# Half tiles for the last rows of an expert in a two-layer transformer kernel

## The chip, the core and the metric

The kernel runs on one core of a Trainium2 chip, as one launch. The metric is the device time of one execution in microseconds (us); the median of three executions stands for a kernel. One further execution was taken with the hardware profiler, and every row of a profile below is from that one.

TensorE is written PE (PEld is its loading of weights, which overlaps its matmuls), VectorE DVE, ScalarE ACT, GpSimd POOL, and SP is the engine that only issues DMAs. All data are float32, and a float32 matmul shows in the profile as two passes.

## The reference

Two sequences of 2048 tokens with 256 features go through two layers. What matters here is the mixture of experts in layer 0, which sees the normalised tokens `xn`:

```python
scores = softmax(x @ gate_w + gate_b)                 # 8 experts
weights, indices = top_k(scores, 2)                   # two experts for each token
p1 = x @ rw1[e] + rb1[e]                              # 256 -> 512, for each chosen expert e
p2 = x @ rw2[e] + rb2[e]
routed_e = (silu(p1) * p2) @ rw3[e] + rb3[e]          # 512 -> 256
out = shared(x) + sum(weights * routed_e over the two chosen)
```

Around it stand a causal attention of layer 0, two shared experts of the same form, and in layer 1 another causal attention and a block that works on 255 chosen tokens of each sequence. There are 4096 tokens, so 8192 pairs of a token and an expert; how many fall to one expert depends on the data.

## The kernel before

**Layer 0's attention, with side work.** `attention` goes over 32 blocks of 128 query rows. Scores are made by L251 and scaled by DVE in L262, the exponential is ACT's L270, POOL splits each row into two 16-bit planes (L301), SP transposes them by DMA (L303, tile `across`), DVE and ACT join them again (L281, L282), and L316 multiplies by the values. Beside it runs side work, a generator: each `yield` in it is one step, and `beside()` takes steps at a set rate per piece of attention. `behind` ties POOL's DMAs of the side work to DVE's last main instruction, so that they don't come in a burst. The DMAs that clear buffers in DRAM (`clear`, issued by ACT at L420 to L442, biases packed last) are taken one or two per block of rows.

**Planning (`route_experts`, side work).** DVE finds the two best experts of each token. Two matmuls (L537, L538) count the rows of each expert. From the counts (`many`, `last`, L549 to L557) each expert gets `ceil(rows / 256)` tiles of `TT = 256` rows, one behind the other in a DRAM buffer `sorted_x`, and each pair gets its place there (`place`, L565). `tile_expert` (L574) holds the expert of each tile, and `filled` (L575) the number of tiles. Then 64 indirect DMAs of POOL (L580) scatter the tokens' rows to their places.

**Expert tiles (`fetch` and `run`).** At most `NT = 39` tiles can be needed. `LIKELY = 36` of them are run always, the other 3 in one block under `tc.If(used > LIKELY)` (L773). For each tile `fetch` has SP load the tile's expert number into a register (L622), transpose the tile's rows from DRAM (L626, `xs`), and load the expert's weights (L631, three `rw` tiles of 512 KB) and biases (L635, `be`), whatever expert the tile before had. These tiles have two buffers each, and `chained` keeps SP's DMAs of all tiles in one order. `run` then has POOL put the two 16-bit halves together (L730, `xT`), multiplies into `ps_sc` and `ps_tr` (L737: two groups `h`, in each two matmuls per 128 hidden features and projection), applies Silu on ACT (L745), multiplies on DVE (L746, `hid`), multiplies by the third weight (L752: two blocks of 128 rows, four matmuls each), adds the bias (L757, `y`) and stores to `sorted_y` (L758). From the twelfth tile on ACT loads one later weight behind each tile (L767), and behind one of the last tiles four small products for layer 1 are made (L706).

**After the tiles** come the shared experts (L1370, L1389) with the gathering of the routed rows from `sorted_y` by indirect DMA (L1359), then layer 1.

## Time and profile before

| | us |
|---|---|
| three executions | 1529.97, 1533.32, 1532.8 |
| their median | 1532.8 |
| profiled execution, its own time | 1530.43 |
| its span on the core | 1528.7 |
| PE busy | 1474.6 |
| first matmul of the expert tiles to the first of the shared experts | 378.5 |

The span is the stretch from the first to the last recorded instruction; the rest of an execution's time lies around it. The mean granted clock of PE is 0.996 of full. In groups of instructions a matmul's length covers its way through the array, and the next one starts before it ends; what counts for PE is the distance from start to start. A row of DMAs gives the size of one and the median time from issue to landing:

```profile
rw<-in_rw SPq DMA_DIRECT2D x108, 512.0 KB, 4.3
be<-biases SPq DMA_DIRECT2D x36, 132.0 KB, 4.2
xs<-sorted_x SPq DMA_TRANSPOSE x36, 3.4
```

### The profile page before, as it was taken

What the parts mean: (1) busy time and instruction counts of PE and PEld (TensorE: products, weight loads), DVE (VectorE), ACT (ScalarE), POOL (GpSimd) and SP (SyncE); (2) the same over time, 40 slices, a digit from 0 to 9 for tenths busy, and PEclk for the clock granted to TensorE, in tenths of its full rate; (3) what the DMA queues carried; (4) which work ended last, traced back from release to release, by engine and by line L of the source; (5) the groups of instructions that cost most, each with busy time, mean ns of one, the idle gap of its engine ahead of it and who ended that gap; (6) DMA issues with size and microseconds to landing.
All of it is one profiled execution on the core that took longest, in us unless ns stands there. A gap on an engine that the chain in (4) does not pass through costs nothing.

```text
span 1528.7 us, 17889 instructions
## 1 busy us (share of the span) xinstructions
PE 1474.6 (96%) x5828; PEld 1047.4 (69%) x5828; DVE 698.3 (46%) x2055; ACT 442.1 (29%) x831; POOL 409.4 (27%) x596
## 2 busy tenths in 40 slices
PE   7999999999999999999999999999999998999998
PEld 4566666568888888888556566566675765676665
DVE  6446333342222222222334446767546458666344
ACT  2443343341111111111121211115623532354233
POOL 3555776431111111110112220132012122421132
PEclk9999999999999999999999999999999999999999
DMA  4944765656888879874110110130005435621144
GB/s 150 268 107 116 174 137 134 158 119 175 212 218 231 238 234 270 237 202 122 30 40 28 42 42 21 37 135 28 1 14 111 109 67 114 151 52 23 35 114 103
DMA packets 290558, 183.49 MB, mean 120 GB/s; under 512 B 192960, under 2 KB 265408, under 8 KB 290464
## 3 DMA queue, kind: packets, MB, share of 16 engines
q1 hardware_dynamic: 255168, 134.95, 35.7%
q10 hardware_dynamic: 27664, 26.53, 5.5%
q0 software_dynamic: 7632, 20.86, 4.4%
q8 instruction: 47, 0.77, 0.2%
q14 instruction: 47, 0.39, 0.1%
HBM read 93.14 MB, written 45.14 MB: 90 GB/s over the span
## 4 chain that ended last, share of the span: by engine, by line
PE 28%; issue 9%; DVE 7%; POOL 3%; DMA 3%; ACT 2%; SPq 0%; POOLq 0%; ACTq 0%; DVEq 0%
PE ps_tr L1370 6%; PE ps_sc L1370 6%; PE ps_pv L1389 5%; POOL planes L301 3%; DMA across<-planes 2%; PE ps_mm L1241 2%; PE ps_mm L1203 1%; DVE x L1400 1%; PE ps_sc L251 1%; PE ps_mm L833 1%; PE ps_mm L1224 1%; PE ps_pv L316 1%; PE ps_tr L251 1%; PE ps_mm L1307 1%; DVE row L262 1%
## 5 line engine op out<-in xcount | busy, mean ns | idle before, releaser
L301 POOL COPY planes<-row 128x512 uint16<-128x512 uint16 (+3 forms) x320 | 166.6, 565 | 304.9 <-ACT row L270 279.1
L282 ACT COPY pT<-across 128x512 uint16<-128x512 uint16 (+3 forms) x160 | 105.9, 676 | 214.7 <-DMA across<-planes 204.5
L251 PE MATMUL ps_sc<-xnT,qT 128*128 128x512 f32 (+3 forms) x384 | 161.6, 542 | 0.1
L746 DVE SCALAR_TENSOR_TENSOR hid<-ps_tr,be,act 128x256 f32<-128x256 f32 x144 | 63.1, 480 | 197.9 <-PE ps_tr L737 188.9
L745 ACT ACTIVATE act<-ps_sc,be 128x256 f32<-128x256 f32 x144 | 60.5, 471 | 302.0 <-PE ps_sc L737 302.0
L1359 POOL DMA_INDIRECT ya<-sorted_y,place x64 | 62.3, 974 | 308.1 <-DVE x L1400 224.7
L737 PE MATMUL ps_sc<-xT,rw 128*128 128x256 f32 x576 | 136.2, 379 | 1.6 <-POOL xT L730 1.6
L737 PE MATMUL ps_tr<-xT,rw 128*128 128x256 f32 x576 | 136.1, 379 | 0.0
L316 PE MATMUL ps_pv<-v,pT 128*128 128x256 f32 x544 | 129.6, 384 | 5.9 <-ACT pT L282 4.5
L730 POOL COPY xT<-xs 128x512 uint16<-128x512 uint16 x72 | 51.3, 758 | 309.7 <-DMA xs<-sorted_x 269.9
L752 PE MATMUL ps_pv<-rw,hid 128*128 128x256 f32 x576 | 132.0, 382 | 0.0
L316 PE MATMUL ps_pv<-vg,pT 128*128 128x256 f32 x544 | 124.9, 380 | 5.0 <-ACT pT L282 4.9
L1370 PE MATMUL ps_tr<-xnT,sw 128*128 128x512 f32 x256 | 122.0, 593 | 0.0
L1370 PE MATMUL ps_sc<-xnT,sw 128*128 128x512 f32 x256 | 121.9, 594 | 0.1
L316 PEld LDWEIGHTS ps_pv<-vg,pT 128*128 128x128 f32 x544 | 101.5, 189 | 28.9 <-ACT pT L282 9.5
L316 PEld LDWEIGHTS ps_pv<-v,pT 128*128 128x128 f32 x544 | 101.7, 191 | 28.3 <-ACT pT L282 8.4
L737 PEld LDWEIGHTS ps_sc<-xT,rw 128*128 128x128 f32 x576 | 109.4, 190 | 16.8 <-POOL xT L730 2.0
L737 PEld LDWEIGHTS ps_tr<-xT,rw 128*128 128x128 f32 x576 | 109.4, 190 | 14.9
L752 PEld LDWEIGHTS ps_pv<-rw,hid 128*128 128x128 f32 x576 | 104.9, 189 | 21.2 <-DVE hid L746 6.6
L1389 PE MATMUL ps_pv<-sw,hid 128*128 128x256 f32 x512 | 117.7, 380 | 0.0
L1389 PEld LDWEIGHTS ps_pv<-sw,hid 128*128 128x128 f32 x512 | 96.5, 190 | 19.1 <-issue 6.2
L251 PEld LDWEIGHTS ps_sc<-xnT,qT 128*128 128x128 f32 x384 | 70.4, 191 | 53.6 <-issue 43.3
(319 smaller groups left out, 1936.1 us busy)
## 6 DMA issues: line engine op xcount, KB each, us to landing
rw<-in_rw SPq DMA_DIRECT2D x108, 512.0 KB, 4.3
sorted_x<-zero ACTq DMA_DIRECT2D x13, 768.0 KB, 6.5
sorted_y<-y SPq DMA_DIRECT2D x36, 256.0 KB, 4.3
be<-biases SPq DMA_DIRECT2D x36, 132.0 KB, 4.2
table<-xn SPq DMA_DIRECT2D x8, 514.0 KB, 3.4
x<-in_x SPq DMA_DIRECT2D x8, 512.0 KB, 6.7
gains<-zero ACTq DMA_DIRECT2D x8, 512.0 KB, 3.4
gain<-gains SPq DMA_DIRECT2D x16, 256.0 KB, 2.7
```

The source lines that it names most:

```text
L251: product = nc.tensor.matmul(ps[:, :w], lhsT=qT[:, dc, (i % 4) * P : (i % 4 + 1) * P], rhs=xnT[g0 + k][:, dc, :w], start=(dc == 0), stop=( ...
L282: nc.scalar.copy(words[:, :, 0], flat[:, w : 2 * w]),
L301: nc.gpsimd.tensor_copy(planes[:, h * w : (h + 1) * w], halves[:, :, 1 - h])
L316: product = nc.tensor.matmul(pv[:, :D], lhsT=turned[k][:, j : j + P], rhs=values[g0 + k][:, j // P, :D], start=(c + j == 0), stop=(c + j = ...
L730: nc.gpsimd.tensor_copy(words[:, :, :, 1 - k], xs[:, 2 * k : 2 * k + 2, :])
L737: nc.tensor.matmul(ps[:, k * TT : (k + 1) * TT], lhsT=we_in[:, dc, (h + k) * P : (h + k + 1) * P], rhs=xT[:, dc, :], start=(dc == 0), stop ...
L745: activated = nc.scalar.activation(act, p1[:, at], AF.Silu, bias=b1[:, hc])
L746: nc.vector.scalar_tensor_tensor(hid[:, h + k, :], p2[:, at], b2[:, hc], act, op0=ALU.add, op1=ALU.mult)
L752: product = nc.tensor.matmul(po[:, r, :], lhsT=hid[:, hc, r * P : (r + 1) * P], rhs=w3[:, hc, :], start=(hc == 0), stop=(hc == 3),)
L1359: nc.gpsimd.indirect_dma_start(out=ya, out_offset=None, in_=sorted_y, in_offset=bass.IndirectOffsetOnAxis(ap=place[rank][:, t : t + 1], ax ...
L1370: product = nc.tensor.matmul(ps, lhsT=ww[:, dc, hc * P : (hc + 1) * P], rhs=xnT[g][:, dc, :], start=(dc == 0), stop=(dc == 1),)
L1389: product = nc.tensor.matmul(po[:, :D], lhsT=hid[:, hc, j * P : (j + 1) * P], rhs=w["sw3", n][:, hc, :], start=(hc == 0), stop=(hc == 3),)
```

## The change

An expert's rows are cut into whole tiles of 256; a remainder of more than 128 rows gets a whole tile, and one of 1 to 128 rows gets a half tile of `HT = 128`. Whole tiles come first in `sorted_x`, half tiles behind all of them from row `NT * TT`. At most 35 whole and 8 half tiles can be needed; the buffers keep their 9984 rows. 32 whole and 4 half tiles are run always, the half ones behind the 5th, 13th, 21st and 29th whole one. The 3 other whole and 4 other half tiles stand in one conditional block, which runs all seven if there are more than 32 whole or more than 4 half tiles. A half tile runs the same instructions on 128 columns, with one block of rows in place of two at the third weight; its weights and biases are loaded in full. Planning gets the instructions that find the half tiles and move their rows' places, and one more `yield`; clearing `sorted_y` takes two DMAs where it took one.

```diff
-NT = (2 * B * S + E * (TT - 1)) // TT
-LIKELY = 2 * B * S // TT + E // 2
+HT = TT // 2
+NT, NH = (2 * B * S + E * (HT - 1)) // TT, E
+LIKELY, LIKELY_H = 2 * B * S // TT, E // 2
+PLACES = NT * TT + NH * HT
...
-            for r in range(LIKELY * TT, NT * TT, step):
+            for r, end in ((LIKELY * TT, NT * TT), (NT * TT + LIKELY_H * HT, PLACES)):
...
-            nc.vector.tensor_sub(many, at[:, 1:], at[:, :E])
-            nc.vector.tensor_scalar(
-                many, many, 1.0 / TT, (TT - 1.0) / TT - 0.5 + 0.5 / TT, op0=ALU.mult, op1=ALU.add
-            )
+            nc.vector.tensor_sub(count, at[:, 1:], at[:, :E])
+            nc.vector.tensor_scalar(many, count, 1.0 / TT, -0.5 / TT, op0=ALU.mult, op1=ALU.add)
...
+            nc.vector.scalar_tensor_tensor(half, many, -float(TT), count, op0=ALU.mult, op1=ALU.add)
+            nc.vector.tensor_scalar(half, half, 0.0, None, op0=ALU.is_gt)
             nc.vector.tensor_tensor_scan(last, many, many, 0.0, ALU.add, ALU.max)
+            nc.vector.tensor_tensor_scan(half_last, half, half, 0.0, ALU.add, ALU.max)
+            nc.vector.tensor_sub(jump, half_last, half)
+            nc.vector.tensor_scalar(jump, jump, float(HT), float(NT * TT), op0=ALU.mult, op1=ALU.add)
+            nc.vector.scalar_tensor_tensor(jump, last, -float(TT), jump, op0=ALU.mult, op1=ALU.add)
...
+            nc.vector.tensor_scalar(count, last, float(TT), None, op0=ALU.mult)
...
+            yield
+            nc.vector.tensor_tensor(total, summed, each_expert(count), ALU.is_ge)
+            nc.vector.tensor_tensor(total, total, each_expert(jump), ALU.mult)
+            nc.vector.tensor_tensor(summed, summed, total, ALU.add)
...
-            nc.vector.tensor_copy(filled, last[:, E - 1 :])
+            nc.vector.tensor_scalar(one[:, 0:1], last[:, E - 1 :], -float(LIKELY), 0.0, op0=ALU.add, op1=ALU.max)
+            nc.vector.tensor_scalar(one[:, 1:2], half_last[:, E - 1 :], -float(LIKELY_H), None, op0=ALU.add)
+            nc.vector.tensor_tensor(filled, one[:, 0:1], one[:, 1:2], ALU.max)
...
+        def place_of(t):
+            return (t * TT, TT) if t < NT else (NT * TT + (t - NT) * HT, HT)
...
-            part = slice(t * TT, (t + 1) * TT)
+            first, n = place_of(t)
...
-                                ps[:, k * TT : (k + 1) * TT],
+                                ps[:, k * n : (k + 1) * n],
...
-            for r in range(2):
+            r_n = n // P
+            for r in range(r_n):
...
-        for t in range(LIKELY):
+        every_so = LIKELY // LIKELY_H
+        planned = []
+        for t in range(LIKELY):
+            planned.append(t)
+            if t % every_so == every_so // 2:
+                planned.append(NT + t // every_so)
+        for at, t in enumerate(planned):
             product, activated = run(t)
...
-        with tc.If(used > LIKELY):
-            for t in range(LIKELY, NT):
+        with tc.If(used > 0):
+            for t in [*range(LIKELY, NT), *range(NT + LIKELY_H, NT + NH)]:
                 run(t)
```

More of the change, by code (lines that the diff above doesn't have):

```diff
@@ L54, in transformer_kernel @@
     dram = ctx.enter_context(tc.tile_pool(name="scratch", bufs=2, space=bass.MemoryType.DRAM))
-    sorted_x = dram.tile([NT * TT, 2 * D], U16, tag="sorted_x", name="sorted_x", bufs=1)
-    sorted_y = dram.tile([NT * TT, D], F32, tag="sorted_y", name="sorted_y", bufs=1)
+    sorted_x = dram.tile([PLACES, 2 * D], U16, tag="sorted_x", name="sorted_x", bufs=1)
+    sorted_y = dram.tile([PLACES, D], F32, tag="sorted_y", name="sorted_y", bufs=1)
     gains = [dram.tile([S + 1, D], F32, tag=f"gains{b}", name=f"gains{b}", bufs=1) for b in range(B)]
@@ L353, in transformer_kernel @@
     gate = [keep_pool.tile([P, NB * 4], F32, tag=f"gate{k}", name=f"gate{k}") for k in range(2)]
-    tile_expert = keep_pool.tile([P, NT], I32, tag="tile_expert", name="tile_expert")
+    tile_expert = keep_pool.tile([P, NT + NH], I32, tag="tile_expert", name="tile_expert")
     filled = keep_pool.tile([P, 1], I32, tag="filled", name="filled")
@@ L418, in clear @@
             step = 3 * TT
-            for r in range(0, NT * TT, step):
+            for r in range(0, PLACES, step):
                 yield nc.scalar.dma_start(
@@ L423, in clear @@
                 )
-            for r in range(LIKELY * TT, NT * TT, step):
+            for r, end in ((LIKELY * TT, NT * TT), (NT * TT + LIKELY_H * HT, PLACES)):
                 yield nc.scalar.dma_start(
-                    sorted_y[r : r + step, :].rearrange("(p r) d -> p r d", p=P),
-                    zero.bitcast(F32).unsqueeze(1).to_broadcast([P, step // P, D]),
+                    sorted_y[r:end, :].rearrange("(p r) d -> p r d", p=P),
+                    zero.bitcast(F32).unsqueeze(1).to_broadcast([P, (end - r) // P, D]),
                 )
@@ L546, in route_experts @@
             nc.vector.tensor_copy(at[:, 1:], summed[:, :, n - 1])
-            many, last = (plan.tile([P, E], F32, tag=t, name=t) for t in ("many", "last"))
-            nc.vector.tensor_sub(many, at[:, 1:], at[:, :E])
-            nc.vector.tensor_scalar(
-                many, many, 1.0 / TT, (TT - 1.0) / TT - 0.5 + 0.5 / TT, op0=ALU.mult, op1=ALU.add
-            )
+            count, many, last, half, half_last, jump = (
+                plan.tile([P, E], F32, tag=t, name=t) for t in ("count", "many", "last", "half", "half_last", "jump")
+            )
@@ L558, in route_experts, with each_expert @@
             nc.vector.tensor_sub(sflat, sflat, tflat)
             nc.vector.tensor_tensor(sflat, sflat, ps[:, : E * n], ALU.add)
-            nc.vector.tensor_tensor(summed, summed, many.unsqueeze(2).to_broadcast([P, E, n]), ALU.add)
+            def each_expert(t):
+                return t.unsqueeze(2).to_broadcast([P, E, n])
+            nc.vector.tensor_tensor(summed, summed, each_expert(many), ALU.add)
+            yield
+            nc.vector.tensor_tensor(total, summed, each_expert(count), ALU.is_ge)
@@ L565, in route_experts @@
                 nc.vector.tensor_copy(place[rank], one)
-            tiles = plan.tile([P, NT, E], F32, tag="tiles", name="tiles")
-            nc.gpsimd.iota(
-                tiles, pattern=[[1, NT], [0, E]], base=0, channel_multiplier=0, allow_small_or_imprecise_dtypes=True
-            )
-            nc.vector.tensor_tensor(tiles, tiles, last.unsqueeze(1).to_broadcast([P, NT, E]), ALU.is_ge)
-            whose = plan.tile([P, NT], F32, tag="whose", name="whose")
+            tiles = plan.tile([P, NT + NH, E], F32, tag="tiles", name="tiles")
+            for part, n_of, ends in ((tiles[:, :NT, :], NT, last), (tiles[:, NT:, :], NH, half_last)):
+                nc.gpsimd.iota(
+                    part, pattern=[[1, n_of], [0, E]], base=0, channel_multiplier=0,
+                    allow_small_or_imprecise_dtypes=True,
+                )
+                nc.vector.tensor_tensor(part, part, ends.unsqueeze(1).to_broadcast([P, n_of, E]), ALU.is_ge)
+            whose = plan.tile([P, NT + NH], F32, tag="whose", name="whose")
             nc.vector.tensor_reduce(whose, tiles, AX.X, ALU.add)
             nc.vector.tensor_scalar(tile_expert, whose, float(E - 1), None, op0=ALU.min)
-            nc.vector.tensor_copy(filled, last[:, E - 1 :])
+            nc.vector.tensor_scalar(one[:, 0:1], last[:, E - 1 :], -float(LIKELY), 0.0, op0=ALU.add, op1=ALU.max)
+            nc.vector.tensor_scalar(one[:, 1:2], half_last[:, E - 1 :], -float(LIKELY_H), None, op0=ALU.add)
+            nc.vector.tensor_tensor(filled, one[:, 0:1], one[:, 1:2], ALU.max)
             yield
@@ L625, in fetch @@
             yield
-            turn = lambda: nc.sync.dma_start_transpose(xs, sorted_x[t * TT : (t + 1) * TT, :])
+            first, n = place_of(t)
+            turn = lambda: nc.sync.dma_start_transpose(
+                xs.rearrange("p c n -> p (c n)")[:, : 4 * n].rearrange("p (c n) -> p c n", n=n),
+                sorted_x[first : first + n, :],
+            )
             if t > 1:
@@ L719, in run @@
         def run(t):
-            part = slice(t * TT, (t + 1) * TT)
+            first, n = place_of(t)
             if t not in fetched:
@@ L725, in run @@
             b1, b2, b3 = be[:, 0:4], be[:, 4:8], be[:, 8:]
-            xT = hp.tile([P, 2, TT], F32, tag="xT", name="xT", bufs=3)
+            xs = xs.rearrange("p c n -> p (c n)")[:, : 4 * n].rearrange("p (c n) -> p c n", n=n)
+            xT = hp.tile([P, 2, TT], F32, tag="xT", name="xT", bufs=3)[:, :, :n]
             words = xT.bitcast(U16).rearrange("p c (n k) -> p c n k", k=2)
@@ L730, in run @@
                 nc.gpsimd.tensor_copy(words[:, :, :, 1 - k], xs[:, 2 * k : 2 * k + 2, :])
-            hid = hp.tile([P, 4, TT], F32, tag="hid", name="hid")
+            hid = hp.tile([P, 4, TT], F32, tag="hid", name="hid")[:, :, :n]
             for h in range(0, 4, 2):
@@ L742, in run @@
                 for k in range(2):
-                    act = hp.tile([P, TT], F32, tag="act", name="act", bufs=3)
-                    at, hc = slice(k * TT, (k + 1) * TT), slice(h + k, h + k + 1)
+                    act = hp.tile([P, TT], F32, tag="act", name="act", bufs=3)[:, :n]
+                    at, hc = slice(k * n, (k + 1) * n), slice(h + k, h + k + 1)
                     activated = nc.scalar.activation(act, p1[:, at], AF.Silu, bias=b1[:, hc])
@@ L755, in run @@
                     )
-            y = hp.tile([P, 2, D], F32, tag="y", name="y", bufs=3)
-            nc.vector.tensor_tensor(y, po, b3.unsqueeze(1).to_broadcast([P, 2, D]), ALU.add)
-            nc.sync.dma_start(sorted_y[part, :].rearrange("(r p) d -> p r d", p=P), y)
+            y = hp.tile([P, 2, D], F32, tag="y", name="y", bufs=3)[:, :r_n, :]
+            nc.vector.tensor_tensor(y, po[:, :r_n, :], b3.unsqueeze(1).to_broadcast([P, r_n, D]), ALU.add)
+            nc.sync.dma_start(sorted_y[first : first + n, :].rearrange("(r p) d -> p r d", p=P), y)
             return product, activated
         coming = later_weights()
+        every_so = LIKELY // LIKELY_H
+        planned = []
         for t in range(LIKELY):
+            planned.append(t)
+            if t % every_so == every_so // 2:
+                planned.append(NT + t // every_so)
+        for at, t in enumerate(planned):
             product, activated = run(t)
-            if t >= LIKELY // 3:
+            if at >= len(planned) // 3:
                 for dst, src in (next(coming, (None, None)),):
@@ L768, in transformer_kernel @@
                         tc.add_manual_dep(i.ins, activated.ins.name, order, reason="behind a tile")
-            if t == LIKELY - 8:
+            if at == len(planned) - 8:
                 layer1_products(product)
```

## The prediction

> **What bounds the kernel now.** I read the page first (busy shares), then the table by stretches, then the timeline of one expert tile. The page's line of engines:

> ```profile
> PE 1474.6 (96%) x5828; PEld 1047.4 (69%) x5828; DVE 698.3 (46%) x2055; ACT 442.1 (29%) x831; POOL 409.4 (27%) x596
> ```

> TensorE is the bound of the whole: 1474.6 of 1528.7 us. The change touches two stretches, so the table by stretches is cut there: three of 10 us around the planning in layer 0 (L542 to L575), and the expert tiles from their first matmul to the shared experts' first. Columns: busy us and count of PE, PEld, DVE, ACT, POOL, then granted clock, DMA share, GB/s.

> ```profile
> 120.00:130.00 10.00, 9.05 (x37) 6.51 (x36) 9.33 (x26) 4.29 (x8) 5.33 (x8) 1.00 0.49 118
> 130.00:140.00 10.00, 10.00 (x37) 6.90 (x37) 9.55 (x36) 1.74 (x3) 3.26 (x5) 1.00 0.20 62
> 140.00:150.00 10.00, 10.00 (x34) 6.16 (x33) 3.95 (x12) 5.07 (x7) 7.93 (x9) 1.00 0.73 199
> 346.02:724.50 378.48, 378.48 (x1744) 326.77 (x1744) 88.14 (x181) 62.51 (x147) 50.05 (x72) 1.00 0.77 216
> ```

> For 378.5 us the expert tiles keep PE busy without a gap at full granted clock: 36 tiles, and 3.45 us for the products of L706. Whatever matmul time goes, goes from the end. The timeline of one tile (start, length, engine, line) shows what a tile is made of:

> ```profile
> 439.82 1.89 PE L737 MATMUL ps_sc<-xT,rw 128*128 128x256 f32 x8
> 441.54 1.89 PE L737 MATMUL ps_tr<-xT,rw 128*128 128x256 f32 x8
> 443.27 1.89 PE L737 MATMUL ps_sc<-xT,rw 128*128 128x256 f32 x8
> 445.00 1.89 PE L737 MATMUL ps_tr<-xT,rw 128*128 128x256 f32 x8
> 446.72 3.67 PE L752 MATMUL ps_pv<-rw,hid 128*128 128x256 f32 x16
> 450.23 1.89 PE L737 MATMUL ps_sc<-xT,rw 128*128 128x256 f32 x8
> ```

> A tile is 10.41 us (450.23 - 439.82): 32 passes of the first two projections (each matmul of L737 is two passes) in 6.90 us, 0.216 each from start to start, and 16 passes of the third in 3.51 us, 0.219 each. The 379 ns of the groups' rows are lengths that overlap; the sum goes by starts.

> **The change, part by part.** First, how many tiles run. Counting the two choices of each token from the reference's inputs gives 222, 85, 3776, 132, 1896, 1982, 88 and 11 rows per expert. Before, rounded up to 256 each, that is 36 tiles (the page has 108 loads of rw, three per tile, so the conditional block did not run). After, remainders of 1 to 128 (85, 104, 88, 11) become half tiles: 1+0+15+1+7+8+0+0 = 32 whole and 4 half. Both fit exactly what always runs, so four whole tiles become four half ones and the block is skipped again.

> *A half tile.* L737 streams 128 columns instead of 256, L752 loses one of its two row blocks but still streams 256. No expert tile of before has 128 columns. The nearest row is layer 0's score matmul of that shape, same float32, same 128x128 weights, another weight for each matmul:

> ```profile
> 59.20 0.61 PE L251 MATMUL ps_tr<-xnT,qT 128*128 128x128 f32 x4
> 59.64 1.04 PE L229 MATMUL ps_mm<-ident,xn 128*128 128x128 f32 x8
> 60.51 0.59 PE L251 MATMUL ps_sc<-xnT,qT 128*128 128x512 f32 x1
> ```

> Four passes take 0.44 us (59.64 - 59.20), so 0.110 each, and the eight transposes 0.87, so 0.109. A half tile is 32 x 0.110 + 8 x 0.219 = 3.52 + 1.75 = 5.27 us, and saves 10.41 - 5.27 = 5.14; four save 20.6 us. The other end of the price is the duration of a weight load, 190 ns in the groups' rows: were loads to follow one another without overlap, a half tile would be 32 x 0.190 + 1.75 = 7.83 and four save 10.3. I take 0.110, because L251 has those same 190 ns loads and still starts every 0.110.

> [...]

> *Does the feed keep up?* Half the matmuls, but a half tile still loads all of its expert's weights (three of 512 KB, and be). Loads run two tiles ahead. SP's timeline:

> ```profile
> 440.01 0.37 SPq L631 DMA_DIRECT2D rw<-in_rw  x1
> 440.74 0.37 SPq L758 DMA_DIRECT2D sorted_y<-y  x1
> 441.34 0.34 SPq L635 DMA_DIRECT2D be<-biases  x1
> 443.15 1.27 SPq L626 DMA_TRANSPOSE xs<-sorted_x  x1
> 445.19 5.60 SPq L631 DMA_DIRECT2D rw<-in_rw  x3
> ```

> The tightest is be, issued at 441.34 for the tile that starts at 450.23, whose first activation is at 452.16. With its median landing of 4.2 us it is there at 445.5, 6.6 early; a half tile in between takes 5.1 of that and leaves 1.5. The weights issued at 445.19 land by 449.5 for a tile at 460.64, 11 us early, and keep 6. SP's chain from rw3 to the next rw1 is 5.2 us, as long as a half tile; it slips some 0.6 us and the whole tile behind has 5 to spare. The DMA share of whole tiles is about 0.82 of 10.41, 8.5 us of transfer each; a half tile lacks at most 8.5 - 5.3 = 3.2 us, which two whole tiles (1.9 us each) give back, and seven or eight lie between half tiles. So nothing here; without the buffers, a half tile would last 8.5 and four save 7.6.

> *Inside a half tile* the third projection waits for the last hid. Now hid starts 2.00 us after the last group of L737 (445.00 to 447.00). With 8 x 0.106 less streaming and 0.1 less fill it starts about 1.1 after; two vector ops of some 0.35 (estimated between L746's 480 ns for 256 columns and L260's 297 for 128) end at 1.8, needed at 0.88 + 6 x 0.219 = 2.2. No stall; bound 0 to 0.2 each, 0.8 in all.

> *Planning.* Added on DVE: three ops of 128x256 (neighbours L558 to L560: 421, 418, 412 ns), nine small ones (L549 to L557: 160 to 174 ns), 0.2 for the split of L571, together 1.25 + 1.5 + 0.2 = 3.0 us; on POOL one more small iota. DVE has 9.55 of 10 us there, so this pushes its queue back by about 3 us: behind it wait the score rows (L262), the exponentials and the places of the scatter. It has 6 us to spare in the next 10. PE did not wait at all in 130:140 and lost 0.95 in 120:130. Cost 0 to 3.0, below zero not excluded by a little reordering (-1.0); I take 1.0, since the nearest stretch hid the same load and its neighbour lost 0.95.

> *Moved.* One more side step puts the last scatter behind the six plane copies of POOL (289.16 to 292.1), so it lands near 296; SP's first rw load, now at 295.17, waits for it by up to 1 us. Behind it in SP's queue is the next transpose (299.20 now), and xs moves behind that one, so the 4 us between hide it; else 1 us. One more clearing DMA of 512 KB on ACT's queue (0.52 us issue, L431's rows) shifts the last clearing writes by one row block; the last now waits on ACT for be of the second tile, about 317.5, with ACT's next copy at 321.1. Cover gone: 1 us. The branch at L773 jumps over seven tiles rather than three; PE's branch is at 722.7 and its first load behind it at 724.6, under the last tile's matmuls. Zero, at most 1.6.

> **Sum.** The profiled execution takes 1530.43 us (span 1528.7 and 1.7 around it), 2.4 below the median of the runs, 1532.8. 1530.4 - 20.6 + 1.0 = 1510.8, and the same difference from the median: 1513.2.

> **Rivals.** *Starved or load-bound half tiles*: passes at 0.190 (10.3 saved) or weights at 8.5 us (7.6 saved): 1523.5 to 1526.2. For it: 0.82 DMA share and 190 ns loads. Against: L251's starts and loads two tiles ahead. *Slower, the conditional block runs*: the whole fit is exact, 32 and 4. It decides at a fifth half tile or a 33rd whole one; nearest is expert 3, where 132 rows falling to 128 (four tokens going elsewhere) makes a fifth half tile. Then three whole and four half tiles more: 3 x 10.41 + 4 x 5.27 = 52.3, and one load not fetched ahead, about 7 (1.1 register load, 4.3 landing, 1.4 copies): 1513.2 + 59 = 1572. Against it: only one token of expert 3 has its choice within 0.001 of the next in the logits. *Nothing gained*, since the stage is bound elsewhere: 1533; PE's 378.48 of 378.48 speaks against it.

> **Numbers.** Forecast 0.85, starved 0.09, block 0.04, nothing 0.02. About 0.2% (3 us) is what can be told from no change. Faster 0.94, same 0.02, slower 0.04. Low: the lowest run, 1530.0, less 20.6 and 1.0, 1508.4. High: the highest, 1533.3, less 20.6, plus 3.0 planning, 0.8 stall, 1.6 branch, 2.0 queues, 1520.1.

> **What would show it.** Right: 32 tiles at 10.41 and four near 5.3 from start to start, L737 with 128 columns starting every 0.11, the stage near 358 us, PE idle around 130:150 up by 1 or 2 us, 36 loads of each rw. Wrong: 0.19 between those starts, PE waits on DMA behind half tiles, or more than 108 loads of rw.

## The result, and the profile after

The changed kernel takes 1514.94 us in the median of four runs (1513.97 to 1516.8). The kernel before, run beside it, takes 1533.06 (1529.97 to 1536.03). The ratio is 0.9883 with a 95% interval of 0.9861 to 0.9906. The forecast was 1513.2, in a range of 1508.4 to 1520.1.

The profiled execution takes 1515.69 us, with a span of 1513.95. Here is that span against the 1528.73 of before, cut at the first or last matmul of each stage:

| stretch, us | before | after | difference |
|---|---|---|---|
| start to the first expert matmul | 346.02 | 348.54 | +2.5 |
| first to last expert matmul | 378.12 | 357.66 | -20.5 |
| last expert matmul to the first of the shared experts | 0.53 | 2.09 | +1.6 |
| shared experts, with what lies among them | 421.56 | 421.27 | -0.3 |
| behind the last matmul of the shared experts | 382.50 | 384.39 | +1.9 |

The second row is what the prediction was about. The others are small, and the experiments have to say which of them the change made. First the page's line of engines and its row of weight loads:

```profile
PE 1455.0 (96%) x5796; PEld 1032.3 (68%) x5796; DVE 695.7 (46%) x2068; ACT 440.3 (29%) x831; POOL 407.7 (27%) x597
...
rw<-in_rw SPq DMA_DIRECT2D x108, 512.0 KB, 4.5
```

PE lost 32 matmuls, eight for each of four tiles, and 19.6 us of busy time. The 108 loads of rw say that 36 tiles ran and the conditional block did not. The table by stretches, with the columns of the prediction, has the planning and then the stage of the expert tiles:

```profile
120.00:130.00 10.00, 9.82 (x40) 7.14 (x38) 9.34 (x28) 3.51 (x7) 4.51 (x7) 1.00 0.49 118
130.00:140.00 10.00, 9.26 (x35) 6.68 (x36) 9.63 (x40) 2.65 (x4) 3.21 (x6) 1.00 0.16 53
140.00:150.00 10.00, 10.00 (x33) 5.77 (x32) 6.52 (x22) 4.83 (x7) 7.47 (x9) 1.00 0.70 182
348.54:708.29 359.75, 358.04 (x1712) 311.15 (x1713) 85.65 (x182) 60.80 (x147) 47.87 (x72) 1.00 0.80 224
```

In the planning DVE carries on into the third slice (6.52 us busy where it was 3.95), while PE's idle time over the three is 0.92 us against 0.95. In the stage PE is no longer without a gap: 1.71 us are missing. The timeline of a half tile, and the first group of the whole tile behind it (start, length, engine, line):

```profile
400.69 1.05 PE L772 MATMUL ps_sc<-xT,rw 128*128 128x128 f32 x8
401.58 1.06 PE L772 MATMUL ps_tr<-xT,rw 128*128 128x128 f32 x8
402.48 1.06 PE L772 MATMUL ps_sc<-xT,rw 128*128 128x128 f32 x8
403.37 1.06 PE L772 MATMUL ps_tr<-xT,rw 128*128 128x128 f32 x8
404.26 1.89 PE L788 MATMUL ps_pv<-rw,hid 128*128 128x256 f32 x8
405.99 1.89 PE L772 MATMUL ps_sc<-xT,rw 128*128 128x256 f32 x8
```

L772 and L788 are the former L737 and L752. 32 passes take 404.26 - 400.69 = 3.57 us, 0.112 each; eight of L788 take 1.73. The half tile is 5.30 us, four times over, and the whole tiles stay at 10.41. No row has an idle time in brackets: the feed keeps up and hid is in time. The 1.71 us lie at the end of the stage, where the timeline names PE's own sequencer at the branch (L816, the former L773), and all of its instructions at that line give the branch's duration in ns and its start:

```profile
702.91 3.67 PE L788 MATMUL ps_pv<-rw,hid 128*128 128x256 f32 x16
708.29 1.96 PE L1413 MATMUL ps_sc<-xnT,sw 128*128 128x512 f32 x4 [1.71 <-PEq L816]
```

```profile
L816 PEldq COMPARE_BRANCH  x1: 3372/3372/3372, 704.8 to 704.8; - x1
...
L816 PEldq EVENT_SEMAPHORE  x1: 51/51/51, 708.2 to 708.2; - x1
```

Before, the same view of the branch had this, and only 0.15 us of idle time behind it:

```profile
L773 PEldq COMPARE_BRANCH  x1: 367/367/367, 722.7 to 722.7; - x1
L773 PEldq EVENT_SEMAPHORE  x1: 51/51/51, 724.6 to 724.6; - x1
```

The branch over seven tiles takes 3.4 us instead of 0.4. EVENT_SEMAPHORE is the next thing that PE's sequencer, which is ahead of the matmuls (the branch starts at 704.8, the last tile's matmuls run until 706.6), does behind the branch: it comes 3.43 us after the branch's start, and before it came 1.86 us after it, so 1.5 us behind the end of the short branch. The four other engines' branches take 53 to 76 ns in both kernels.

### The profile page after: what moved, and what is told of

It reads as the page before. It is cut to its first block, busy times and chain, and to the rows that moved or that the text cites. A ratio compares the mean times of both kernels' runs of the same rounds, so it can differ in the third digit from the quotient of the medians.

```text
span 1514.0 us, 17838 instructions
## 1 busy us (share of the span) xinstructions
PE 1455.0 (96%) x5796; PEld 1032.3 (68%) x5796; DVE 695.7 (46%) x2068; ACT 440.3 (29%) x831; POOL 407.7 (27%) x597
## 4 chain that ended last, share of the span: by engine, by line
PE 29%; issue 10%; DVE 7%; POOL 3%; DMA 2%; ACT 2%; POOLq 0%; ACTq 0%; DVEq 0%; SPq 0%
PE ps_tr L1413 6%; PE ps_sc L1413 6%; PE ps_pv L1432 5%; POOL planes L305 3%; DMA across<-planes 2%; PE ps_mm L1284 2%; PE ps_mm L1246 1%; DVE x L1443 1%; PE ps_sc L255 1%; PE ps_mm L876 1%; PE ps_mm L1267 1%; PE ps_pv L320 1%; PE ps_mm L1350 1%; DVE row L266 1%; PE ps_tr L255 1%
## 5 line engine op out<-in xcount | busy, mean ns | idle before, releaser
L781 DVE SCALAR_TENSOR_TENSOR hid<-ps_tr,be,act 128x256 f32<-128x256 f32 (+1 forms) x144 | 61.0, 465 | 186.7 <-PE ps_tr L772 181.7
L780 ACT ACTIVATE act<-ps_sc,be 128x256 f32<-128x256 f32 (+1 forms) x144 | 58.8, 459 | 283.3 <-PE ps_sc L772 283.3
L772 PE MATMUL ps_sc<-xT,rw 128*128 128x256 f32 (+1 forms) x576 | 129.5, 368 | 1.6 <-POOL xT L765 1.6
L772 PE MATMUL ps_tr<-xT,rw 128*128 128x256 f32 (+1 forms) x576 | 129.4, 367 | 0.0
L765 POOL COPY xT<-xs 128x512 uint16<-128x512 uint16 (+1 forms) x72 | 49.2, 728 | 293.3 <-DMA xs<-sorted_x 270.7
L788 PE MATMUL ps_pv<-rw,hid 128*128 128x256 f32 x544 | 124.9, 382 | 0.0
L320 PEld LDWEIGHTS ps_pv<-vg,pT 128*128 128x128 f32 x544 | 101.4, 189 | 29.7 <-ACT pT L286 10.3
L772 PEld LDWEIGHTS ps_sc<-xT,rw 128*128 128x128 f32 x576 | 105.3, 190 | 15.4 <-POOL xT L765 2.0
L772 PEld LDWEIGHTS ps_tr<-xT,rw 128*128 128x128 f32 x576 | 105.1, 190 | 13.2
L788 PEld LDWEIGHTS ps_pv<-rw,hid 128*128 128x128 f32 x544 | 99.0, 189 | 19.5 <-DVE hid L781 5.9
L1420 ACT ACTIVATE act<-ps_sc,sb 128x512 f32<-128x512 f32 x64 | 43.9, 686 | 219.5 <-PE ps_sc L1413 206.4
```

The lines of the kernel that those rows point to most:

```text
L320: product = nc.tensor.matmul(pv[:, :D], lhsT=turned[k][:, j : j + P], rhs=values[g0 + k][:, j // P, :D], start=(c + j == 0), stop=(c + j = ...
L765: nc.gpsimd.tensor_copy(words[:, :, :, 1 - k], xs[:, 2 * k : 2 * k + 2, :])
L772: nc.tensor.matmul(ps[:, k * n : (k + 1) * n], lhsT=we_in[:, dc, (h + k) * P : (h + k + 1) * P], rhs=xT[:, dc, :], start=(dc == 0), stop=( ...
L780: activated = nc.scalar.activation(act, p1[:, at], AF.Silu, bias=b1[:, hc])
L781: nc.vector.scalar_tensor_tensor(hid[:, h + k, :], p2[:, at], b2[:, hc], act, op0=ALU.add, op1=ALU.mult)
L788: product = nc.tensor.matmul(po[:, r, :], lhsT=hid[:, hc, r * P : (r + 1) * P], rhs=w3[:, hc, :], start=(hc == 0), stop=(hc == 3),)
```

## The experiments

Ratios are to the kernel before, run beside each on the same chip; "gap" is the time from the last expert matmul to the first shared one, "tail" the stretch behind the last matmul of the shared experts, "stage" the second row of the table.

### The changed kernel once more

> The changed kernel once more, beside the others on the same chip. If the saving is the four half tiles less what planning and the longer branch give back (20.5 - 1 to 2.5 - 1.6), it stands 16.5 to 18 us under the kernel before. If the 14.7 us between the two profiled spans is the true size, 14 to 15. In the profile: PE's branch behind the tiles again near 3.4 us, PE idle 1.7 us there; the first expert matmul 1 to 2.5 us later than before.

1514.49 us (1512.98 to 1517.07, five runs), ratio 0.9887 (0.9867 to 0.9907). Stage 357.69, gap 2.34, PE's branch 3612 ns, tail 384.0. The tiles start at 348.35, as late as in the first profile. The median is 17.2 us under that of the kernel before, inside the 16.5 to 18 of the theory. So the gap belongs to the program, and single runs of it spread over 4 us.

### Half tiles computed at 256 columns

```diff
...
-            first, n = place_of(t)
+            first, n = place_of(t)[0], TT
...
+            kept = place_of(t)[1]
...
+                sorted_y[first : first + kept, :].rearrange("(r p) d -> p r d", p=P), y[:, : kept // P, :]
...
```

The first edit stands in `fetch` and in `run`; of the 256 rows the first 128 are stored.

> Planning, order of tiles, clearing and the block of seven as changed, but the four half tiles load and multiply 256 columns again and only their storing keeps 128 rows (the other rows belong to the next half tile and are thrown away). This leaves the price of all that the change adds. Theory: slower than the kernel before by planning (1 to 2.5 us) and the branch (1.6 us), so 1535.5 to 1537. Rival, the additions cost nothing and the half tiles simply save less than 20.5: 1533, and the block's branch then shows no wait. Rival, the four tiles at other places disturb the feed: any tile but the one behind which L706's products stand takes more than 10.41 us.

1537.46 us (1534.21 to 1541.73, twelve runs), ratio 1.0035 (1.0019 to 1.005). The stage is 378.10 again, to 0.02 us that of before: the columns alone make the saving. The rest of the change is still in it and costs: PE's branch takes 3492 ns and the gap is 2.22. The tail is 388.5, 6 us longer than before, which the branch can't explain, and planning doesn't show: the tiles start at 345.7 (346.0 before). So the median is slower by about as much as the theory said, but the 1 to 2.5 us that the theory gave to planning lie in the tail.

### Without the conditional block

```diff
-        used = chained(lambda: nc.values_load(filled[0:1, 0:1], min_val=0, max_val=NT))
-        with tc.If(used > 0):
-            for t in [*range(LIKELY, NT), *range(NT + LIKELY_H, NT + NH)]:
-                run(t)
```

The block's seven tiles are left out, which this data does not need. Run twice, the second time for the tail.

> The conditional block is left out altogether (with these inputs it never runs). Theory, the jump over the longer block makes PE wait: no PE idle between the last tile and the shared experts, 1.6 to 2.1 us under the changed kernel. Rival, the wait is something else that stands there in any case (the loading of the shared experts' first weights, ACT's and DVE's wait for SP): the gap of PE stays within 0.5 us of 1.7 and the time is that of the changed kernel.

> The changed kernel without its conditional block, once more, for the stretch behind the last shared expert (382.5 us before, 384.4 and 384.0 in the two runs of the changed kernel, 389.1 in the first run without the block). If the longer stretch belongs to the program, as it is laid out, it is 388 to 390 us again and the median stays near 1514.4. If it was an accident of one execution, it is 382 to 385 us, the profiled span is near 1509.5, and the median over these runs should fall below 1513.

1514.41 us (1510.32 to 1516.15) and 1512.65 us (1509.49 to 1518.91), five runs each; ratios 0.988 (0.9859 to 0.9901) and 0.987 (0.9846 to 0.9893). The gap is 0.21 and 0.22 us: without the block PE doesn't wait. But in the first profile the tail was 389.1 us, which gave the gain away, and in the second it was 385.2. The program was the same, so 4 us of the tail are one execution against another.

### A shorter block in the changed kernel

```diff
-            for t in [*range(LIKELY, NT), *range(NT + LIKELY_H, NT + NH)]:
+            for t in range(LIKELY, NT):
```

> The changed kernel with only the three whole tiles in the conditional block (its four half tiles are left out, which this data does not need). If TensorE's branch is dear because of how much code it jumps over, it falls from 3372 ns to the 367 ns of before, TensorE's idle time ahead of the shared experts from 1.7 us to under 0.5, and the gap from the last expert matmul to the first shared one from 2.1 to 0.5 us. If half tiles ahead of the block are what matters, it stays at 3.4 us. The time: 1514.5 - 1.6 = 1512.9 us if the stretch behind the shared experts stays at 384 us, 1517 to 1518 if it takes the 389 us that the kernel without a block showed.

1513.19 us (1510.89 to 1514.62, four runs), ratio 0.9873 (0.9858 to 0.9888). PE's branch:

```profile
L816 PEldq COMPARE_BRANCH  x1: 368/368/368, 702.2 to 702.2; - x1
```

The gap is 0.53 us, exactly that of before, the stage 357.68, the tail 384.4. The wait is gone with the length of the block alone. In the medians that is 1.3 to 1.8 us, as expected, but the intervals overlap.

### A longer block in the kernel before

Four more whole tiles stand in its block, which is still jumped over; no half tiles anywhere. Run twice.

```diff
-            for t in range(LIKELY, NT):
+            for t in [*range(LIKELY, NT), *range(LIKELY - 4, LIKELY)]:
+                fetched.pop(t, None)
```

> The kernel before, with four further whole tiles in its conditional block, which does not run: only the code that is jumped over grows, from three tiles to seven. Theory, the length of the jump sets the price: PE's branch grows from 0.37 to 3 us or more, PE is idle 1.5 to 2 us behind the last tile, and the time rises by that, 1534.5 to 1535. Rival, the wait in the changed kernel comes from its half tiles or its order: the branch stays at 0.37 us and the time at 1533.

> The kernel before with seven whole tiles in the conditional block, once more. TensorE's branch again near 3.5 us and the gap ahead of the shared experts near 2.2 us. The first time its median was 7.8 us above the kernel before, of which the gap explains 1.7 us; the stretch behind the last shared expert was 388.9 us instead of 382.5. If that longer stretch belongs to this program, it is 388 to 390 us again and the median 1538 to 1541 us; if it was an accident, the stretch is 382 to 385 us and the median 1534 to 1536 us.

1539.85 us (1537.79 to 1543.69, five runs) and 1537.54 us (1536.22 to 1541.4, nine runs); ratios 1.0062 (1.0037 to 1.0087) and 1.0036 (1.002 to 1.0053). The branch of the first:

```profile
L773 PEldq COMPARE_BRANCH  x1: 3505/3505/3505, 722.3 to 722.3; - x1
```

3352 ns in the second; gaps 2.23 and 2.10. So the wait needs no half tile. Together with the block of three: the code that the branch jumps over makes the wait, in both kernels and both ways. But the gap explains only 1.6 to 1.7 us of 4 to 8. The tail was 388.9 and 390.9 us, long both times. The second run is nearest to the expectation by which it belongs to this program.

### The kernel before without its block

```diff
-        used = chained(lambda: nc.values_load(filled[0:1, 0:1], min_val=0, max_val=NT))
-        with tc.If(used > LIKELY):
-            for t in range(LIKELY, NT):
-                run(t)
```

> The kernel before without its conditional block of three tiles (jumped over with this data). By the branch alone next to nothing: the gap ahead of the shared experts falls from 0.53 to 0.2 us, so 1531.5 to 1532 us. If the stretch behind the shared experts is longer in every program without a block, it rises from 382.5 to about 389 us and the time to 1537 to 1538.

1532.28 us (1529.44 to 1534.88, eleven runs), ratio 0.9997 (0.9986 to 1.0009). Gap 0.22, tail 384.7. A block of three that is jumped over costs 0.31 us of the gap and nothing that can be told in the time, and a program without a block has no long tail for that reason.

### Two blocks instead of one

Three whole tiles in one block and four half tiles in another, each behind a register and a condition of its own (`filled` gets two columns for the two counts):

```diff
...
+        for k, more in enumerate((range(LIKELY, NT), range(NT + LIKELY_H, NT + NH))):
+            used = chained(lambda: nc.values_load(filled[0:1, k : k + 1], min_val=0, max_val=NT))
+            with tc.If(used > 0):
+                for t in more:
+                    run(t)
```

> The block of seven tiles becomes two, one of the three whole tiles and one of the four half ones, each with its own count and branch; nothing else changes. Theory, the length of the jump sets PE's branch: both branches are as short as the kernel before's 0.37 us, both hidden under the last tile's matmuls, 1.0 to 1.6 us under the changed kernel. Rival, every jump over code that isn't fetched costs some 3 us whatever its length: two of them, 3 us or more over the changed kernel. Rival, what a branch costs is the meeting of the engines behind it: 1 to 3 us over the changed kernel.

1512.48 us (1511.62 to 1514.85, five runs), ratio 0.9881 (0.9861 to 0.9901): no different from the changed kernel. Both of PE's branches (shortest, median and longest in ns):

```profile
L819 PEldq COMPARE_BRANCH  x2: 367/772/1177, 700.4 to 702.9; - x2
```

Each is shorter, but the second begins at 702.89, 2.5 us behind the first, and PE still idles 2.01 us: gap 2.39. Of the 2.5 us, 1.86 pass until PE's sequencer goes on behind the first branch, as in the kernel before, and the rest goes into the second count's register. Behind the second branch it goes on 1.24 us after its start. Cutting the block in two does not remove the wait.

### All four half tiles together

```diff
-            if t % every_so == every_so // 2:
-                planned.append(NT + t // every_so)
+            if t == every_so // 2:
+                planned += [NT + k for k in range(LIKELY_H)]
```

> The four half tiles one behind the other behind the fifth whole tile, nothing else changed. Theory, a half tile has 8.5 us of loads for 5.3 us of matmuls and lives on loads two tiles ahead: the first one or two are hidden, then PE waits for weights or be, some 3.2 us for each further one, 4 to 9 us over the changed kernel, with PE waiting on rw or be among the half tiles. Rival, loads have more room than the DMA share says: no wait, the time of the changed kernel within 1 us.

1515.37 us (1512.77 to 1519.52, four runs), ratio 0.99 (0.9876 to 0.9923). From start to start the four take 5.30, 5.30, 5.49 and 7.89 us. The stage is 360.55, 2.9 us longer, less than the 4 to 9 expected, and the median can't be told from that of the changed kernel. This is the starved tile that the prediction priced, in the timeline behind the fourth half tile:

```profile
416.47 1.99 PE L788 MATMUL ps_pv<-rw,hid 128*128 128x256 f32 x8
420.72 1.97 PE L772 MATMUL ps_sc<-xT,rw 128*128 128x256 f32 x8 [2.26 <-DMA rw<-in_rw]
```

The loads ahead cover two half tiles in full and a third nearly; only then do the weights come late.

### Every tile a half tile

The second 128 rows of each whole tile are not computed; the result of the first is stored in their place.

```diff
-            return (t * TT, TT) if t < NT else (NT * TT + (t - NT) * HT, HT)
+            return (t * TT, HT) if t < NT else (NT * TT + (t - NT) * HT, HT)
...
```

> Every tile computes only its first 128 rows (the other 128 rows of a whole tile are left out, and its result is stored twice), with all its weights still loaded: what does a half tile cost when nothing stands between half tiles? Theory: the loads bind, 7 to 8.5 us from tile to tile, 36 tiles in 250 to 305 us in place of 360, some 1405 to 1460 us in all. Rival, matmuls bind: 5.3 us from tile to tile, 36 tiles in 195 us, 1345 to 1355 us in all.

1442.93 us, one run. The stage is 286.62 us, 8.0 per tile and not 5.3; PE's waits in it:

```profile
PE ps_pv L788 <- DVE hid L781: 48.5, 29, 3.4
PE ps_sc L772 <- DMA rw<-in_rw: 14.6, 14, 1.7
PE ps_tr L772 <- DMA rw<-in_rw: 4.6, 8, 1.0
```

The first names hid, but hid waits for ACT (169.4 of the 177.2 us that L781's row was idle in the whole run), and ACT's row (L780) was idle 235.4 us, 209.9 of them behind the load of be. The transfers bind, at a DMA share of 0.87. Eight us per tile is near the 8.5 that the prediction gave a half tile by its transfers, and the reason why the half tiles stand apart.

### The block made to run

```diff
+            nc.vector.tensor_scalar(filled, one[:, 0:1], 0.0, 1.0, op0=ALU.mult, op1=ALU.add)
```

All seven tiles of the block run, on rows that no token needs.

> The changed kernel with its block of seven made to run (the count that decides is set to 1; the seven tiles work on rows that no token has). This is the price of the rival on the slower side. Theory: 3 x 10.41 + 4 x 5.27 = 52.3 us and one load that is not fetched ahead, about 7, so 55 to 62 us over the changed kernel, slower than the kernel before by some 40. More than 62 if the four half tiles at the end of the block, one behind the other, starve for their weights (up to 10 us more).

1573.48 us (1572.59 to 1574.38, two runs), ratio 1.027 (1.0244 to 1.0295). The stage is 421.53; PE's largest wait there:

```profile
PE ps_sc L773 <- DMA rw<-in_rw: 7.9, 1, 7.9
```

The rival's price was 59 us: 52.3 of tiles and about 7 for the load not fetched ahead. It is 58.5 over the first median of the changed kernel. That is as near as it is by luck: the stage alone is 63.9 us longer, and the gap (0.22), the start and the tail are 1.9, 1.1 and 2.2 shorter in this profile. In the stage the load not fetched ahead costs 8.05 (a tile of 18.46 in place of 10.41) and the tile behind it another 1.84 (12.25); of the four half tiles at the end the third takes 6.25 and the last 5.50 in place of 5.30, so they starve a little, as the expectation allowed.

### What stays open: the tail

Same order of PE's instructions, same work, and 382.2 to 390.9 us. The table by stretches for the tail of the kernel before, and then for that of its copy with a block of seven (second run):

```profile
1146.23:1528.73 382.50, 357.78 (x1416) 243.23 (x1414) 226.78 (x700) 142.34 (x270) 95.91 (x172) 0.99 0.40 88
```

```profile
1148.48:1539.33 390.85, 361.50 (x1416) 244.67 (x1414) 226.44 (x700) 142.33 (x270) 96.88 (x172) 0.98 0.40 86
```

The same 1416 matmuls are 3.7 us longer and PE's idle time is 4.6 us longer (24.7 to 29.3). The first part goes with the granted clock, which falls to one half for 3.4 or 6.8 us at a time.

When it falls can be read from the traces. All changes of the granted clock within one profile lie on a grid of 3.413 us. Cut along that grid, the tails of all fourteen profiles have 1528 windows at full clock. 45 of them are followed by a window at one half, and in each of these 45 PE had idled 1.89 us or more. 1483 are not, and in these PE had idled 1.85 us or less, but for one with 1.90. So a fall goes with PE's idle time within one window. One such place, some 200 us behind the shared experts, in the copy with a block of seven (first run) and in the kernel before, two windows each:

```profile
1349.14:1352.55 3.41, 1.46 (x9) 0.94 (x8) 0.34 (x1) 1.80 (x6) 0.00 (x0) 1.00 0.85 158
1352.55:1355.97 3.42, 3.42 (x10) 2.60 (x9) 2.61 (x5) 0.50 (x2) 0.00 (x0) 0.50 0.00 0
```

```profile
1345.05:1348.46 3.41, 2.29 (x11) 1.67 (x9) 1.61 (x3) 1.96 (x5) 0.81 (x2) 1.00 1.00 187
1348.46:1351.88 3.42, 3.34 (x15) 2.54 (x16) 2.21 (x5) 0.55 (x4) 0.00 (x0) 1.00 0.13 24
```

PE idles 1.95 us of the first window in the one and 1.12 in the other, and the clock falls in the one only. PE waits there for ACT's `pr` (1.20 us in the kernel before), ACT is late by its copies from `across` (there they waited 2.59 and 0.73 us for the DMA), and the first of SP's four transposes into `across` there takes 1.96 us to issue in the one and 1.23 in the other. The half tiles computed at 256 columns and the second run with a block of seven have the same late transpose (2.26 and 1.95) and the same fall; in the other profiles it takes 1.23 to 1.25, and none falls there. Why these programs have it, and where the rest of the tail's idle time comes from, was not found. The clock isn't all of it: the second run without a block lost the least to the clock, mean 1.00 over the tail, and its tail was still 385.2.

## Why the prediction was right, point by point

**The half tile.** Predicted 5.27 us and 20.6 us in all; measured 5.30 and 20.5 (378.12 to 357.66, and 357.66 to 357.70 in all six profiles that keep the half tiles apart and run no tile more). Taking L251's starts instead of the 190 ns of a weight load was the choice that decided it. The trace bears it out: 0.112 us per pass over 32 passes, against 0.110 over L251's four.

**The feed.** Predicted 1.5 us to spare for be; 1.4, 1.8 and 1.9 are left behind three of the four half tiles, and behind the other the landing is not in the trace. The all-half kernel shows that the margin lies in the spacing: with it, nothing waits; without it, 8.0 us per tile.

**Inside the half tile.** No stall, as taken.

**Planning.** Taken as 1.0 us, bounds -1.0 to 3.0; nothing was measured. DVE is pushed back by 2.6 us, as worked out (3.0), but PE's idle time around it did not grow. The expert tiles do start 2.5 us later in the profiled pair, and that looks like a confirmation; it is none. The matmul of L537, ahead of the planning, is already 0.94 late, and six more profiles with this same planning start between 344.6 and 346.6, against 345.6 to 347.1 with the planning of before. What makes the one program start at 348.4, twice, is open. The steps that the prediction lists as moved were taken at nothing, and these starts show no cost of theirs either.

**The branch.** This is the step that failed: "under the last tile's matmuls. Zero, at most 1.6". The reading that PE's branch runs ahead of its matmuls was right (before, it starts at 722.69, and the last tile's matmuls run until 724.52). The 1.6 us between the end of the short branch (723.06) and PE's first load behind it were taken for room in which a longer branch would hide. They were not free: in the three profiles with such a branch PE's sequencer goes on only 1.86 us after its start, and in the kernel before this had already used up the cover, with 0.15 us of idle time behind it. Over seven tiles it goes on 3.41 to 3.67 us after the start, and the difference is what PE idles more: 1.56 us in the first profile of the changed kernel, the upper bound, and 1.81 in the second, above it. The shorter block in one kernel and the longer in the other show that the code in the block is the cause. In the second profile the wait had a further price: PE idled 1.96 us of one window of the clock's 3.413 us grid, the next was at one half, and the shared experts took 423.0 us in place of 421.3.

What PE waits for behind the branch is not shown. The profile has one instruction packet on the DMA queues during the branch of the changed kernel: 16384 bytes, starting 1.0 us into it and 0.93 us long.

```profile
q8 instruction: 1, 0.02, 1.7%
```

That is one packet, 0.02 MB, 1.7% of the DMA engines' time, from 704.7 to 708.2. Before, such a packet starts at 723.81, when the short branch (722.69 to 723.06) is already over. No such packet stands near this place in the three profiles without a block, nor where the block runs and the branch, not taken, lasts 0.09 us. But PE goes on 1.5 us behind the end of the one packet and 0.2 ahead of the end of the other, so its arrival alone doesn't release PE. PE's instructions of three whole tiles are 288 (48 loads and 48 matmuls each), those of the block in the changed kernel 608. The jump over 608 is the dearer one, 3.43 and 3.67 us in its two profiles; but the 1.24 us behind the second of two blocks, with 320 instructions, is less than the 1.86 over 288, so the length isn't all, and where the price rises was not measured.

**The sum.** -20.6 + 1.0 against the median; it came out at -17.9 (1532.8 to 1514.94). The two mis-sized terms, planning at 1.0 instead of 0 and the branch at 0 instead of 1.6, nearly cancel, which is luck. The rest, about 1 us, is within the spread of a run. In the single profiled execution the difference is only 14.7, with the late start and the 1.9 us of tail in it, which no step of the prediction dealt with.

**The rivals.** Starved half tiles exist, but only where several stand together (2.9 us for four) or all tiles are halves. The block that runs was priced at 1572 and takes 1573.5. Nothing gained: the stage is bound by PE, as its 378.48 of 378.48 said.

## What to carry to other kernels

Price a new tile shape by the distance from start to start of the same shape elsewhere in the trace (0.110 us a pass in L251, and 0.112 measured here), not by lengths or by the duration of weight loads (190 ns), and place tiles that are short of matmuls but not of transfers apart from each other (5.30 us each here; one behind the other the fourth took 7.89). The block that is jumped over wasn't free here: with seven tiles of code in place of three PE idled 1.56 and 1.81 us more, at a place where its queued matmuls ran out. Measure the room for it to the engine's next instruction (1.86 us after the start of the short branch), not to the end of the branch (0.37). Compare a difference of a few us by stretches over several profiles before giving it a cause; here one pair of profiles put 2.5 us on a step that costs nothing.

## What the runs showed of the hardware

PE's compare-and-branch takes 0.37 us over three tiles of code and 3.35 to 3.61 us over seven, in seven profiles of five programs; those of the other engines stay at 45 to 76 ns. PE's sequencer goes on 1.86 us and 3.41 to 3.67 us after its start.
